# A joined fc1 chunk, a moved shared product and a reordered QR step in a four-layer block kernel

## The chip, the cores and the metric

The kernel runs on one core of a Trainium2 chip. The metric is the device time of one execution in microseconds (us). Before the change it is 1273.7, the median of three runs (1276.01, 1266.53, 1273.7).

The engines are named as in the profile: PE multiplies matrices and PEld loads its weights, DVE is the vector engine, ACT the scalar engine with its function tables, POOL is GpSimd, and SP issues DMAs. Each runs its instructions in program order and waits on semaphores for the others.

## What is computed

The input x is 32 samples of 128 tokens with 144 features, in f32; `c` is one vector of 144 per sample. Four layers follow each other:

```python
# layer 0: block with adaptive layernorm, q/k layernorm, 16 heads of 9
q, k = ln(q) * g_q, ln(k) * g_k
x = x + g_msa * (softmax(q k^T / 3) v @ w_proj + b_proj)
x = x + g_mlp * (gelu(xn2 @ w1 + b1) @ w2 + b2)        # 576 hidden
# layer 1: rotation
U, _ = qr(P)                                           # P is 144 x 64
R = expm(A(c))                                         # 64 x 64 skew matrix per sample
z = x @ U;  x = x + (z @ R - z) @ U^T
# layer 2: as layer 0, without the q/k layernorm
# layer 3: the same attention, then a mixture of four experts of 576 hidden
cw = softmax of the two largest of xn @ w_gate, else 0
x = x + g_mlp * sum_e cw[e] * (gelu(xn @ w1[e] + b1[e]) @ w2[e] + b2[e])
```

## The kernel before

In the code the blocks are numbered 0 to 2: block 0 is layer 0 ("L0"), block 1 is layer 2 ("L2"), block 2 is layer 3 ("L3"). All four experts are computed for all tokens, in two pairs.

**Tiling.** The 32 samples are 8 groups (NG) of 4 (G). x stays on chip. A contraction over 144 features is one matmul over 128 rows (the *main*) and one over the remaining 16 rows and the bias (the *rest*), which uses only a 32-row tile of PE's array. The rest's moving rows (hR) lie in four row groups, written there by two DMAs (hD, then hR), so that rests with different row tiles can run side by side. `both()` (L717) issues the mains and rests of a few output chunks, rests first or mains first, with a `yield` between the two halves, so that other work can be put there. It serves the q and k products (`qk_chunks`, L754, three chunks), the values, and the first product of each MLP (`fc1`, L1021, 128 of the hidden columns per chunk; five chunks in L0 and L2, nine for a pair of experts, where the last 64 columns of both experts share a chunk named SHARED). After a block of chunks `fc1` says the gelu function once, which loads ACT's table (L1035), and applies gelu to each chunk (L1038). The second product is `mlp2` (through `fc2`, L1044), one sample at a time. In the mixture of experts it is `moe2` and `moe2_parts` (L1204), and a product of the shared chunk (L1210) is done by one of the two experts of a pair for both; `shared_by_gate` multiplies that chunk by the tokens' gates first (L1176). These gates come as rows through a DMA (cwD to cwb), issued by `gate_rows_of` (L1186).

**Attention.** Scores are two products: one (ps_s) only for the row maxima nm (DVE L931), which PE transposes (L871); DVE then puts them beside q (L876), so that the second product (ps_w) comes with the maximum subtracted, and ACT takes its exponential (L935). PE weighs the values (L950), ACT copies the result "on" (L956), and the sums divide it: in blocks 1 and 2 by four DVE instructions (`sums_by_blocks`, L975 to L981), in block 0 by PE transposes and DVE (L963 to L993). Each sample has two halves of scores, n = 0 and n = 1. The scores, the chunks and the rest share seven PSUM banks in a ring; one more holds the weighed values.

**Order.** Nothing schedules at run time. A loop over *ticks* (L1455) advances each block by one sample, and the blocks overlap: block 0 starts at tick 0, block 1 at 35, block 2 at 67. Each tick has named *gaps* between its parts (a, e, t, stats, o, b0, b, den, pre1, c, y1, y2, y3, d, z). `put(tick, gap, f)` hangs work into a gap and `put2` the two halves of a `both` into two gaps (L1344 to L1432); t0 is the first tick of a group. In block 1, a group's MLP is put as three chunks into gap "c" of tick t0+8 and two chunks into gap "c" of t0+9, and mlp2 of its four samples into gaps "b" and "d" of t0+10 and "b" and "c" of t0+11. The q/k chunks of a group are put at its t0-2, gap "c", which is t0+10 of the group three before it. `fill` (L1441) is called at every gap. Besides what was put it runs the layernorm statistics (`ln_stats`, L659 and L660, followed by POOL's variance, L662 ff.), at gap "e" in the ticks of the first block, and two background generators: `prepare_qr` takes Householder QR columns step by step (PE L354, ACT L365, POOL L366, DVE L369 to L380), and `prepare_expm` the matrix exponentials, among them the eight DVE instructions of each half of the series (L568 to L570). The guess, at gap "e" too, is the start of Newton's iteration for the q/k layernorm (DVE L817 and L820, POOL L827 to L830). The residual of attention is formed by DVE (res_a, L1003) and added to x by POOL (L1000).

## Time and profile before

| | |
|---|---|
| median of three runs | 1273.7 us (1266.53 to 1276.01) |
| the profiled execution's own time | 1277.48 us |
| its span | 1275.8 us, mean granted PE clock 0.991 |
| PE busy | 1224.7 us, 13924 matmuls |
| DVE, ACT, POOL busy | 811.5, 781.1, 667.4 us |
| ACT table loads at L935 and L1035 | 57 and 58, 1283 ns each |
| DMA, mean over the span | 48 GB/s |

A profiled execution gives the start and length of every instruction. "Busy" is the time in which an engine has an instruction running; PE's matmuls are pipelined, so that two overlap and a matmul's length is more than its share of PE's time; the distance from one start to the next is that share. In rows of the timeline, "[2.16 <-DVE hid L1176]" says that the engine stood idle for 2.16 us ahead of this instruction, and that DVE's instruction on tile "hid" at line 1176 ended the wait. In rows of the windows, each engine's busy time is followed by its number of instructions, then the granted PE clock (1.00 is full), the share of the DMA engines and GB/s.

The block stages lie in the span as follows: block 0 alone to about 450, block 1 with the end of block 0 from there, blocks 1 and 2 together to about 800, block 2 alone after that, with the last group's experts from about 1200 on.

### The profile page before, as it was taken

How to read it: one execution, taken by the hardware profiler on the slowest of the kernel's cores; microseconds unless marked ns; L12 is line 12 of the kernel's file. 1: busy time of each engine (PE TensorE's matmuls, PEld its weight loads, DVE VectorE, ACT ScalarE, POOL GpSimd, SP SyncE). 2: the span in 40 equal slices, each digit the busy share in tenths (PEclk: the TensorE clock that was granted, in tenths of full speed). 3: DMA queues.
4: the chain of work that ended last, by engine and by line, in shares of the span. 5: the costliest groups of instructions: out<-in, count | busy, mean ns of one | idle time of the engine just before them, and what ended most of it. 6: DMA issues, size and time to landing. Idle time of an engine off the chain costs nothing.

```text
span 1275.8 us, 35335 instructions
## 1 busy us (share of the span) xinstructions
PE 1224.7 (96%) x13924; PEld 895.4 (70%) x13924; DVE 811.5 (64%) x2540; ACT 781.1 (61%) x1732; POOL 667.4 (52%) x1627
## 2 busy tenths in 40 slices
PE   6889898999989999999999999999999999999998
PEld 5668676778767677777777767767676767677666
DVE  4698888876775466676667666646464646455342
ACT  2567767678786665767666667555656565555441
POOL 5567776756664545454545454736362626261600
PEclk9999998999999999999999999999999999999999
DMA  8301011010013211111121111210101010110110
GB/s 220 84 3 38 2 37 37 2 38 18 23 36 124 60 42 38 46 55 35 50 86 55 56 38 47 103 55 27 55 27 55 27 55 30 53 37 17 37 36 17
DMA packets 53144, 60.74 MB, mean 48 GB/s; under 512 B 5200, under 2 KB 36560, under 8 KB 52720
## 3 DMA queue, kind: packets, MB, share of 16 engines
q1 hardware_dynamic: 52320, 58.01, 15.1%
q8 instruction: 112, 1.84, 0.6%
q10 hardware_dynamic: 656, 0.44, 0.2%
q14 instruction: 56, 0.46, 0.1%
HBM read 44.18 MB, written 13.07 MB: 45 GB/s over the span
## 4 chain that ended last, share of the span: by engine, by line
PE 67%; DVE 5%; ACT 1%; DMA 1%; issue 1%; POOL 0%; SPq 0%; DVEq 0%
PE ps_h L722 19%; PE ps_f L1204 9%; PE ps_s L919 6%; PE ps_w L919 6%; PE ps_o L950 6%; PE ps_qk L722 5%; PE ps_f L1044 4%; PE ps_pj L1014 3%; PE ps_v L722 3%; DVE nm L931 2%; PE ps_f L1210 1%; PE ps_o L871 1%; PE ps_hT_m L691 1%; PE ps_hT_a L691 1%; DVE block L979 0%
## 5 line engine op out<-in xcount | busy, mean ns | idle before, releaser
L931 DVE TENSOR_REDUCE nm<-ps_s 128x4 f32<-128x512 f32 x384 | 246.6, 683 | 93.7 <-PE ps_w L919 80.7
L935 ACT ACTIVATE pr<-ps_w 128x512 f32<-128x512 f32 x384 | 208.6, 595 | 145.5 <-PE ps_w L919 136.8
L919 PE MATMUL ps_s<-kT,qT 32*128 32x256 f32 (+2 forms) x1536 | 233.7, 407 | 0.9 <-ACT kT L851 0.9
L919 PE MATMUL ps_w<-q,kT 32*128 32x128 f32 x3072 | 232.5, 285 | 0.0
L919 PEld LDWEIGHTS ps_w<-q,kT 32*128 32x128 f32 x3072 | 196.6, 188 | 10.0 <-issue 6.3
L1038 ACT ACTIVATE hid<-ps_h 128x512 f32<-128x512 f32 (+1 forms) x224 | 120.5, 591 | 91.4 <-PE ps_h L722 91.0
L919 PEld LDWEIGHTS ps_s<-kT,qT 32*128 32x128 f32 x1536 | 137.3, 186 | 29.2 <-issue 9.4
L1214 DVE SCALAR_TENSOR_TENSOR acc<-ps_f,cwz,acc 128x144 f32<-128x144 f32 x128 | 46.7, 365 | 157.4 <-PE ps_f L1204 87.8
L722 PE MATMUL ps_h<-hM_m,mlps 128*128 128x512 f32 x304 | 144.1, 607 | 0.0
L1000 POOL TENSOR_TENSOR x_sb<-x_sb,res_a 128x144 f32<-128x144 f32 x96 | 47.1, 491 | 145.0 <-DVE res_a L1003 144.2
L950 PE MATMUL ps_o<-pr,vaug 128*32 128x128 f32 x3072 | 104.2, 276 | 0.0
L950 PEld LDWEIGHTS ps_o<-pr,vaug 128*32 128x32 f32 x3072 | 78.4, 110 | 32.7 <-PE ps_w L919 14.4
L722 PEld LDWEIGHTS ps_h<-hM_m,mlps 128*128 128x128 f32 x304 | 53.3, 189 | 67.0 <-issue 66.2
L1044 PE MATMUL ps_f<-mlps,hid 128*128 128x144 f32 x640 | 93.7, 294 | 0.0
L1044 PEld LDWEIGHTS ps_f<-mlps,hid 128*128 128x128 f32 x640 | 82.4, 190 | 8.8 <-issue 4.5
L935 ACT ACT_TABLE_LOAD x57 | 73.1, 1283 | 10.0 <-PE ps_w L919 9.1
L794 POOL TENSOR_SCALAR kT<-kT,cst 128x512 f32<-128x512 f32 x30 | 47.0, 1565 | 61.1 <-ACT kT L776 59.7
L662 POOL TENSOR_SCALAR rs_m_a<-mv_m_a 128x2 f32<-128x2 f32 x81 | 17.2, 212 | 114.2 <-DVE mv_m_a L660 86.3
L1204 PEld LDWEIGHTS ps_f<-mlps,hid 128*128 128x128 f32 x512 | 67.3, 190 | 13.5 <-issue 12.2
L1204 PEld LDWEIGHTS ps_f<-pair,hid 128*128 128x128 f32 x512 | 68.7, 193 | 9.7 <-issue 7.9
L1035 ACT ACT_TABLE_LOAD x58 | 74.4, 1283 | 1.0
L1204 PE MATMUL ps_f<-pair,hid 128*128 128x144 f32 x512 | 74.5, 292 | 0.0
(337 smaller groups left out, 2725.8 us busy)
## 6 DMA issues: line engine op xcount, KB each, us to landing
gates<-gates SPq DMA_DIRECT2D x48, 288.0 KB
hD_m<-hG_m SPq DMA_DIRECT2D x24, 256.0 KB
hR_m<-hD_m SPq DMA_DIRECT2D x24, 256.0 KB
hD_a<-hG_a SPq DMA_DIRECT2D x16, 256.0 KB
hR_a<-hD_a SPq DMA_DIRECT2D x16, 256.0 KB
cwb<-cwD SPq DMA_DIRECT2D x32, 128.0 KB
x_sb<-in_x SPq DMA_DIRECT2D x8, 288.0 KB
out_x<-x_sb SPq DMA_DIRECT2D x7, 288.0 KB
```

Of the source, the lines that this page charges most:

```text
L722: nc.tensor.matmul(ps, x, y, start=k == 0, stop=k == 1)
L794: eng.tensor_scalar(o, k, m, None, ALU.mult)
L919: nc.tensor.matmul(o, x, y, start=True, stop=True)
L931: nc.vector.tensor_reduce(to, view, AX.X, ALU.max, negate=True)
L935: nc.scalar.activation(pr[:, 4 * e : 4 * e + 4, :].rearrange("p s q -> p (s q)"), view, AF.Exp, scale=SCALE,)
L950: nc.tensor.matmul(po[rows4(j), t, :], v[:, 4 * j + 2 * t + r, :], prs[j // 2][:, 4 * (j % 2) + 2 * r + t, :], start=r == 0, stop=r == 1,)
L1000: nc.gpsimd.tensor_tensor(x_sb[:, b, :], x_sb[:, b, :], t, ALU.add)
L1035: nc.scalar.activation(t, half, AF.Gelu_apprx_tanh)
L1038: nc.scalar.activation(hid[:n, i], ps[:n], AF.Gelu_apprx_tanh)
L1044: nc.tensor.matmul(ps, hid[:, at0, i, :], w2[:, m, :], start=m == 0, stop=m == NFC - 1)
L1204: nc.tensor.matmul(ps[:, 0, :], hid[:, at0 + m, i, :], w2[:, at0 + m, :], start=m == 0, stop=m == 3)
L1214: nc.vector.scalar_tensor_tensor(acc, ps[:, 0, :], w, acc, ALU.mult, ALU.add)
```

## The change

It has three parts.

1. **First block.** The series' terms of the matrix exponential yield a mark. Where a mark comes at gap "z" of a tick, the next tick is put into `behind`: in that tick, gap "e" is left out, and its work (the statistics and the guess) runs at gap "t", where the pieces of the QR step have come first. This holds in eight ticks, those of QR columns 24, 26, and so on to 40. The instructions are the same; their order on DVE changes there.

2. **fc1 chunks.** A table, MLP_TILES, now gives the row tile of each chunk's rest. `both` has a third form (None): the first half of the mains, all rests, the second half of the mains. In block 1 four chunks are put at t0+8, gap "c", in this form; the fifth is joined with the three q/k chunks three groups ahead, in the same form, at t0+10, gap "c" (JOIN), with its gelu ahead of ACT's copies of q. Nothing is put at t0+9, gap "c". mlp2 goes from gaps b, d, b, c of ticks t0+10, 10, 11, 11 to gaps d, b, c, d of ticks t0+10, 11, 11, 11. In block 2 the second pair of the first five groups goes from 3+3+3 chunks to 4+4 and one that is joined with q/k chunks. All eight groups of block 1 have a joined chunk, which makes 13 joins. The gelu function is said before the products, in place of between them and the gelus, in this form.

3. **Last group.** For pair 0 of the last group the product of the shared chunk is done by the second expert for all four samples (before: by the first for three of them). `shared_by_gate` goes from gap "stats" to "den" there, and the DMA of the gate rows (`gate_rows_of`) from "den" to "pre1" for all groups.

The counts of instructions are the same but for ten more table loads. Weights are laid out on the host by MLP_TILES; that part of the diff is left out here.

```diff
--- before.py
+++ after.py
@@ -25,6 +25,10 @@
 
 SHARED = 8
 NPC = 9
+MLP_TILES = {
+    "L0": (0, 1, 2, 0, 1), "L2": (0, 1, 2, 3, 3),
+    "L3_0": (0, 1, 2, 0, 1, 2, 0, 1, 2), "L3_1": (1, 2, 3, 3, 0, 1, 0, 2, 3),
+}
 MLP_COLS = NFC * (128 + 128 + C)
 PAIR_COLS = NPC * (256 + C)
 D = 64
@@ -341,6 +345,7 @@
     rotU = const.tile([128, NB2, C], F32, name="rotU")
 
     qr_rest = 3 * D
+    SERIES = "series"
 
     def prep_qr():
 
@@ -565,10 +570,10 @@
             lo, hi = mat(f"{name}_lo"), mat(f"{name}_hi", "hi")
             for t, cs_ in ((hi, co[4:]), (lo, co[:4])):
                 nc.vector.tensor_scalar(t, pw1, cs_[1], None, ALU.mult)
-                yield
+                yield SERIES
                 for c, x in ((cs_[0], i2b), (cs_[2], pw2), (cs_[3], pw3)):
                     nc.vector.scalar_tensor_tensor(t, x, c, t, ALU.mult, ALU.add)
-                    yield
+                    yield SERIES
             yield from products(
                 pw4, hi, f"ps_{name}",
                 lambda bs, ps: nc.vector.tensor_tensor(lo[:, bs, :], lo[:, bs, :], ps, ALU.add),
@@ -716,7 +721,16 @@
 
     def both(main, rest, rest_first):
 
-
+        if rest_first is None:
+            n = len(main) // 2
+            for ps, x, y in main[:n]:
+                nc.tensor.matmul(ps, x, y, start=True, stop=False)
+            for k, (ps, x, y) in enumerate(rest):
+                nc.tensor.matmul(ps, x, y, start=k >= n, stop=k < n)
+            yield
+            for ps, x, y in main[n:]:
+                nc.tensor.matmul(ps, x, y, start=False, stop=True)
+            return
         for k, products in enumerate((rest, main) if rest_first else (main, rest)):
             for ps, x, y in products:
                 nc.tensor.matmul(ps, x, y, start=k == 0, stop=k == 1)
@@ -751,19 +765,31 @@
             gr[g]["kT"] = take_kT()
         return gr[g]["qT"], gr[g]["kT"]
 
+    JOIN = {(1, n): (1, n - 3) for n in range(3, NG)}
+    JOIN.update({(2, n): (1, n + NG - 3) for n in range(3)})
+    JOIN.update({(2, n): (2, n - 3) for n in range(3, NG)})
+
     def qk_chunks(g):
 
 
         p = PARAMS[g[0]]
         hM, hR = gr[g]["hM_a"], gr[g]["hR_a"]
         qT, kT = qk_tiles(g)
+        f = JOIN.get(g)
+        if f is not None:
+            l, mlp, m = ("L2", MLPS[1], 4) if f[0] == 1 else ("L3_1", PAIRS[1], 3)
+            name = f"{f[0]}_{f[1]}_s"
+            gelu_table(name, m)
+            psh, main, rest = fc1_products(f, l, mlp, name, (m,))
+        else:
+            main, rest = [], []
         pss = [bank([128, G * T], f"ps_qk_{g[0]}_{g[1]}_{m}") for m in range(3)]
         cols = [slice(128 * m, 128 * m + 128) for m in range(3)]
-        yield from both(
-            [(ps, p.wqk[:, c], hM) for ps, c in zip(pss, cols)],
-            [(ps, p.wqkR[rows4(m), cols[m]], hR[rows4(m)]) for m, ps in enumerate(pss)],
-            False,
-        )
+        main += [(ps, p.wqk[:, c], hM) for ps, c in zip(pss, cols)]
+        rest += [(ps, p.wqkR[rows4(m), cols[m]], hR[rows4(m)]) for m, ps in enumerate(pss)]
+        yield from both(main, rest, False if f is None else None)
+        if f is not None:
+            gelus(f, psh, (SHARED,))
         nc.scalar.copy(qT[:, 0, :], pss[0])
         if g[0] == 1 and g[1] < 2:
             nc.gpsimd.tensor_copy(kT[:, 3, :], kmask[:, 3:4].to_broadcast([128, G * T]))
@@ -1018,21 +1044,30 @@
         layer, b, g, i = of(s)
         residual(b, st[s].pop("pj"), gr[g]["ga"][:, i, :], f"a_{s}", layer == 0)
 
-    def fc1(g, p, name, m, to, rest_first):
-
+    def fc1_products(g, l, p, name, ms):
 
         hM, hR = gr[g]["hM_m"], gr[g]["hR_m"]
-        pss = [bank([128, G, T], f"ps_h_{name}_{m + i}") for i in range(len(to))]
-        cols = [slice(128 * (m + i), 128 * (m + i) + 128) for i in range(len(to))]
-        tiles = [rows4((m + i) % 3) for i in range(len(to))]
-        yield from both(
-            [(ps, p.w1[:, c], hM) for ps, c in zip(pss, cols)],
-            [(ps, p.w1R[r, c], hR[r]) for ps, c, r in zip(pss, cols, tiles)],
-            rest_first,
-        )
-
+        pss = [bank([128, G, T], f"ps_h_{name}_{m}") for m in ms]
+        cols = [slice(128 * m, 128 * m + 128) for m in ms]
+        tiles = [rows4(MLP_TILES[l][m]) for m in ms]
+        main = [(ps, p.w1[:, c], hM) for ps, c in zip(pss, cols)]
+        rest = [(ps, p.w1R[r, c], hR[r]) for ps, c, r in zip(pss, cols, tiles)]
+        return pss, main, rest
+
+    def fc1(g, l, p, name, ms, to, rest_first):
+        if rest_first is None:
+            gelu_table(name, ms[0])
+        pss, main, rest = fc1_products(g, l, p, name, ms)
+        yield from both(main, rest, rest_first)
+        if rest_first is not None:
+            gelu_table(name, ms[0])
+        gelus(g, pss, to)
+
+    def gelu_table(name, m):
         t = small.tile([128, 1], F32, tag="gelu", name=f"gelu_{name}_{m}", bufs=1)
         nc.scalar.activation(t, half, AF.Gelu_apprx_tanh)
+
+    def gelus(g, pss, to):
         for ps, i in zip(pss, to):
             n = 64 if g[0] < 2 and i == SHARED else 128
             nc.scalar.activation(hid[:n, i], ps[:n], AF.Gelu_apprx_tanh)
@@ -1045,7 +1080,8 @@
         return ps
 
     def mlp1(g, m, to, rest_first):
-        return fc1(g, MLPS[g[0]], f"{g[0]}_{g[1]}", m, to, rest_first)
+        ms = range(m, m + len(to))
+        return fc1(g, ("L0", "L2")[g[0]], MLPS[g[0]], f"{g[0]}_{g[1]}", ms, to, rest_first)
 
     def mlp2(g, i):
         b = g[1] * G + i
@@ -1166,8 +1202,11 @@
                 nc.gpsimd.tensor_tensor(acc, acc, t, ALU.add)
 
     def moe1(g, pair, part, rest_first):
-        to = ((0, 1, 2), (SHARED, 3, 4), (5, 6, 7))[part]
-        return fc1(g, PAIRS[pair], f"3_{g[1]}_{pair}", 3 * part, to, rest_first)
+        ms = range(3 * part, 3 * part + 3)
+        if part > 2:
+            ms = ((0, 1, 2, 4), (5, 6, 7, 8))[part - 3]
+        to = [(0, 1, 2, SHARED, 3, 4, 5, 6, 7)[m] for m in ms]
+        return fc1(g, f"L3_{pair}", PAIRS[pair], f"3_{g[1]}_{pair}", ms, to, rest_first)
 
     def shared_by_gate(g, pair):
 
@@ -1205,7 +1244,7 @@
                 ps[:, 0, :], hid[:, at0 + m, i, :], w2[:, at0 + m, :], start=m == 0, stop=m == 3
             )
         yield
-        shared = e % 2 == (i == 0)
+        shared = e % 2 == (i == 0 or (g[1], e // 2) == (NG - 1, 0))
         if shared:
             nc.tensor.matmul(
                 ps[:, 1, :], hid[:, SHARED, i, :], w2[:, SHARED, :], start=True, stop=True
@@ -1303,11 +1342,16 @@
         elif prep_last and next(prep_last, 0) == 0:
             load_late()
 
+    behind = set()
+
     def prepare_expm(tick, gap):
         nonlocal prep_expm
         if prep_expm and (tick >= 0 and gap in ("b", "z") or (tick, gap) == (-2, "z")):
             said = next(prep_expm, 0)
-            if said == 0:
+            if said is SERIES:
+                if gap == "z":
+                    behind.add(tick + 1)
+            elif said == 0:
                 prep_expm = None
             elif said is not None:
                 rot_T.append(said)
@@ -1399,27 +1443,31 @@
                     at_ = t0 + 12 + i // 2 + ((n, i) == (NG - 1, G - 1))
                     put(at_, "bd"[i % 2] if at_ < first[1] or (n, i) == (NG - 2, G - 1) else "bc"[i % 2], mlp2, g, i)
             elif layer == 1:
-                put2(t0 + 8, "c", "c", mlp1, g, 0, (0, 1, 2), True)
-                put2(t0 + 9, "c", "c", mlp1, g, 3, (3, SHARED), True)
+                put2(t0 + 8, "c", "c", mlp1, g, 0, (0, 1, 2, 3), None)
                 for i in range(G):
-                    put(t0 + (10, 10, 11, 11)[i], "bdbc"[i], mlp2, g, i)
+                    put(t0 + (10, 11, 11, 11)[i], "dbcd"[i], mlp2, g, i)
             else:
                 put2(t0 + 7, "o", "c", gate_logits, g)
                 put(t0 + 8, "e", expert_ranks, g)
                 put(t0 + 8, "stats", expert_weights, g)
                 put(t0 + 8, "den", gate_rows, g)
-                put(t0 + 9, "den", gate_rows_of, g, 1)
+                put(t0 + 9, "pre1", gate_rows_of, g, 1)
                 for i in range(G):
                     put(t0 + 8 + i // 2, "cdab"[i], moe_bias, g, i, n == NG - 1)
                 for pair in range(2):
                     at_ = t0 + 8 + 2 * pair
-                    put2(at_, "stats", "b0", moe1, g, pair, 0, True)
+                    if pair and n < NG - 3:
+                        put2(at_, "stats", "b0", moe1, g, pair, 3, None)
+                        put2(at_ + 1, "stats", "b0", moe1, g, pair, 4, None)
+                    else:
+                        put2(at_, "stats", "b0", moe1, g, pair, 0, True)
                     if n == NG - 1:
                         put2(at_, "stats", "pre1", moe1, g, pair, 1, True)
-                    else:
+                    elif not pair or n >= NG - 3:
                         put2(at_, "den", "pre1", moe1, g, pair, 1, False)
-                    put2(at_ + 1, "stats", "b0", moe1, g, pair, 2, True)
-                    put(at_ + 1, "stats", shared_by_gate, g, pair)
+                    if not pair or n >= NG - 3:
+                        put2(at_ + 1, "stats", "b0", moe1, g, pair, 2, True)
+                    put(at_ + 1, "den" if (n, pair) == (NG - 1, 0) else "stats", shared_by_gate, g, pair)
                     put2(at_, "y2", "y3", moe2_parts, g, 2 * pair, 0)
                     put(at_ + 1, "b", moe2, g, 2 * pair, 1)
                     put(at_ + 1, "c", moe2, g, 2 * pair, 2)
@@ -1445,7 +1493,12 @@
             prepare_qr(tick, gap)
             prepare_expm(tick, gap)
 
-        if gap == ("t" if tick < 0 else "e" if tick < first[1] else "stats") and tick in stats:
+        if gap == "e" and tick in behind:
+            return
+        if gap == "t" and tick in behind:
+            gaps[tick, "t"] = gaps.pop((tick, "e"), []) + gaps.pop((tick, "t"), [])
+        at_head = "t" if tick < 0 or tick in behind else "e"
+        if gap == (at_head if tick < first[1] else "stats") and tick in stats:
             ln_stats(stats.pop(tick))
         for f, args in gaps.pop((tick, gap), ()):
             f(*args)
...
```

## The prediction

> **What bounds the kernel now.** I read the page first: TensorE's share, then the chain of work that ended last.
>
> ```profile
> PE 1224.7 (96%) x13924; PEld 895.4 (70%) x13924; DVE 811.5 (64%) x2540; ACT 781.1 (61%) x1732; POOL 667.4 (52%) x1627
> ...
> PE 67%; DVE 5%; ACT 1%; DMA 1%; issue 1%; POOL 0%; SPq 0%; DVEq 0%
> ```
>
> 96% is an average, so next the windows by stage (length, then busy us of PE, PEld, DVE, ACT, POOL, granted clock, DMA):
>
> ```profile
> 50.00:250.00 200.00, 180.95 (x2414) 139.80 (x2413) 173.29 (x579) 139.14 (x402) 144.24 (x403) 0.97 0.09 27
> 250.00:450.00 200.00, 192.49 (x2612) 146.00 (x2612) 135.10 (x459) 145.16 (x363) 113.60 (x333) 0.98 0.15 48
> 450.00:600.00 150.00, 149.24 (x1876) 108.44 (x1874) 101.15 (x292) 96.35 (x189) 73.67 (x158) 1.00 0.15 44
> 750.00:1200.00 450.00, 447.88 (x4458) 317.85 (x4455) 247.47 (x735) 262.55 (x492) 221.26 (x461) 1.00 0.15 47
> ```
>
> From 450 on PE stands still for under 1%: there only less PE work can save, and every new wait of PE costs in full. In the first block DVE is the busier partner (87% in 50 to 250), and PE waits for it.
>
> Sums go against the profiled execution: 1277.48 us, span 1275.8, 3.8 above the median of 1273.7.
>
> **Part 1, layer 2's MLP on PE.** By starts in PE's rows, a 512-column main matmul is two passes of 0.43, a main-to-rest switch 0.52, rest matmuls of one row tile 0.52 a pass, and rests on other tiles follow 0.006 apart. So a fourth rest on a free tile is nearly free. Per group, before: three chunks 3.74, two chunks 2.88, the q/k chunks 4.04: 10.66. After: two blocks of four mains. One is 0.20 + 0.53 + 2 x 0.43 + 0.52 + 0.52 + 0.52 + 0.53 + 3 x 0.43 = 4.98, two are 9.96. PE work falls by 0.7 a group, 5.6 in eight.
>
> But the two-chunk block stood in gap "c" of tick t0+9, and nothing comes there now. Behind that gap PE transposes nm, the negated row maxima. This tick in group 2, PE's rows, then DVE's, then ACT's:
>
> ```profile
> 599.38 0.28 PE L919 MATMUL ps_w<-q,kT 32*128 32x128 f32 x2
> 599.49 1.02 PE L722 MATMUL ps_h<-hR_m,mlps 32*128 32x512 f32 x4
> 600.44 1.98 PE L722 MATMUL ps_h<-hM_m,mlps 128*128 128x512 f32 x4
> 602.26 0.27 PE L871 MATMUL ps_o<-cst,nm 128*128 128x128 f32 x1
> ```
> ```profile
> 598.27 0.45 DVE L975 STREAM_TRANSPOSE block<-on 128x256 f32<-128x256 f32 x1
> ...
> 599.86 1.28 DVE L931 TENSOR_REDUCE nm<-ps_s 128x4 f32<-128x512 f32 x2
> ```
> ```profile
> 595.60 1.28 ACT L935 ACT_TABLE_LOAD   x1 [0.85 <-PE ps_w L919]
> 596.89 1.09 ACT L935 ACTIVATE pr<-ps_w 128x512 f32<-128x512 f32 x2
> 597.86 0.38 ACT L956 COPY on<-ps_o 128x256 f32<-128x256 f32 x1
> ```
>
> The scores end at 599.4, nm at 601.14. The two chunks (599.49 to 602.26) hid that. The chain is table load, two exps, the copy of "on", four DVE instructions (1.6) and two reductions (1.28); the change shortens none of it. Without the chunks PE waits for it: from the end of the scores to the end of nm I read 1.76 in groups 0 to 3, 2.31 in group 4, and 2.72, 2.79, 2.79 in groups 5 to 7, where layer 3 shares the engines.
>
> The rest of the group: the chunk taken out returns as one more in tick t0+8 and one in t0+10 (counted above); the mlp2 steps move one gap later each, 1.23 out of t0+10 and into t0+11, net nothing. A 0.35 wait for q, seen now behind t0+8, is then covered. Lowest to highest the wait costs 0 (if nm is done with the scores) to 2.8; I take the readings.
>
> The joined chunk needs the q/k layernorm's transposed rows (hR_a, two DMAs on SP's queue). They land 1.4 to 2.9 before use (609.11 against 611.84, 753.84 against 755.26). In t0+10 the use comes 2.1 earlier: 1.24 of mlp2 is gone, and one main of 0.86 no longer lies ahead. ACT, which feeds it, is 0.3 to 0.6 earlier. So between 0 and 1.4 a group; I take 0.5.
>
> The first gelu of a joined chunk puts its table load and 0.59 of gelu ahead of ACT's copies of q: hidden while scores stand 2 us and more away, up to 1.3 a group if not. The exp load of t0+10 moves to t0+11, the same count in this layer.
>
> Per group: -0.7 + 1.76 - 0.35 + 0.5 + 0.1 = +1.3 in groups 0 to 3, +1.9 in group 4, +2.3 in 5 to 7. Sum **+14.0**.
>
> **Part 2, layer 3.** Five groups' second pair goes from 3+3+3 chunks to 4+4 and one joined. By the same passes 0.2 less each: **-1.0**. Its two more table loads a group (2.6 on ACT) lie in stretches where ACT is 58% busy; if they were bare, +13, if hidden 0; I take 0, since ACT waits 91 us for the chunks in front of its gelus.
>
> **Part 3, the first block.** In eight ticks (QR columns 24 to 40, every second) six DVE instructions of the QR step go ahead of two pairs of statistics and two of the guess. The tick of column 36, DVE, POOL, then PE:
>
> ```profile
> 210.11 0.30 DVE L1003 TENSOR_TENSOR res_a<-ps_pj,gates 128x144 f32<-128x144 f32 x1
> ...
> 211.77 0.15 DVE L369 SCALAR_TENSOR_TENSOR ala<-qrr,qr 128x1 uint32<-128x1 uint32 x1
> ```
> ```profile
> 210.49 0.49 POOL L1000 TENSOR_TENSOR x_sb<-x_sb,res_a 128x144 f32<-128x144 f32 x1 [0.23 <-DVE res_a L1003]
> 210.94 0.55 POOL L366 TENSOR_TENSOR qr<-qr,half 128x1 f32<-128x1 f32 x1
> ```
> ```profile
> 213.60 0.82 PE L354 MATMUL ps_qr<-at,cst 128*128 128x145 f32 x2 [2.44 <-DVE at L380]
> ```
>
> The step starts with L369, which needs POOL's power (L366). That stands in POOL's queue behind the residual add (L1000), which waits for DVE's res_a. It ends about 1.1 after res_a; the step starts 1.36 after it. The statistics and the guess (1.43) fill that hole. After the change the step can start only 0.27 earlier, DVE stands idle 1.1, and everything then behind the step (statistics, guess, the nm reductions, POOL's variance at L662) comes some 1.05 later, all queued on DVE. PE's next scores want the bank that nm frees: by each tick's slack PE loses 0.95, 0.6, 1.0, 1.09 and 1.09 in five, nothing in three: 4.7. PE's waits ahead of ps_qr (0.91, 1.93, 2.44 in three of these ticks) shrink by 0.27 each at most, which is within it. Bounds: -5.3 (all three waits gone) to +8.4 (1.05 in all eight). I take **+4.7**.
>
> **Part 4, the tail.** For the last group the shared product moves to the second expert, its gating to a later gap.
>
> ```profile
> 1242.50 0.51 PE L1210 MATMUL ps_f<-pair,hid 128*128 128x144 f32 x2 [2.16 <-DVE hid L1176]
> ```
> ```profile
> 1243.66:1247.07 3.41, 3.41 (x16) 3.41 (x15) 1.45 (x5) 0.00 (x0) 0.00 (x0) 0.50 0.23 82
> ```
>
> DVE's L1176 waited for the rows of cwb until 1241.75. Afterwards three first-expert products (0.98 each) fill the time, so the wait goes: -2.2. The half clock behind it (3.41 at 0.50, so 1.65 lost) should go too: **-3.8**. Next late is nothing that I see: the gated rows are then ready at 1242.4, before 1243.
>
> **The clock.** PE's rows show 0.50 for a 3.4 us window at 165.05, 212.84, 325.5, 383.5 and 1243.66, each after a window in which PE was busy for 1.25 to 1.87 of 3.41. A new wait of 1.8 to 2.8 in each of eight groups can do the same if it falls within one window; each costs 1.7 at most, all eight 13.6, none 0. I take two to three, **+4**, as only the larger waits reach it.
>
> The Trainium skill ("TensorE: Matmul & The Clock Gate", "Why this matters for your kernels") speaks of idle gaps of more than about 3 us; by that sentence no new wait here trips the clock, and the sum would be 4 lower, 1288. The trace disagrees: 0.50 followed single idle stretches of 1.9 to 2.4 us.
>
> **Sum.** 14.0 - 1.0 + 4.7 - 3.8 + 4 = +17.9. On 1277.5 that is 1295.4; less the 3.8 by which the profiled execution stands above the median, **1291.5**.
>
> **The rivals.**
> - *The gap costs nothing.* If nm were ready within 0.3 us of the scores in tick t0+9 (the DVE queue drained earlier, the exps earlier), the saved passes count in full: layer 2 -5.6, layer 3 -1, tail -3.8, first block 0 to +4.7: 1263 to 1268. It decides from a wait under 0.7. For it: DVE has 64% load overall. Against it: DVE's four block instructions and the reductions run back to back behind "on", without idle. Not slower. Chance 0.20.
> - *The first block's step helps.* The QR step starts earlier, PE's three waits go (-5.3) and nm is not late: 10 less than my sum, 1281.5. Against it: POOL's power is not earlier. As far as its start is concerned the change then does not do what it says. Chance 0.13.
> - *The clock drops in every tick t0+9*, and hR_a is late by 1.4 in all groups: +9.6 and +7.2, 1301 to 1308. For it: the waits are of the size that went before 0.50. Against: windows end anywhere in them. Chance 0.15.
>
> **How the numbers follow.** My own forecast has chance 0.52, with its own range 1284 to 1299. The range over all, 1267 to 1306, leaves out half of the first rival and the edge of the third. Under 1% a measurement of this kernel can hardly tell from no change: below 1261 is faster, above 1286.4 slower. Faster: the deep end of the first rival, 0.05. Within 1%: the rest of it, the second rival and the lower edge of my own, 0.35. Slower: 0.60.
>
> **What would show it.** Right: PE rows of the nm transpose (L871) in tick t0+9 waiting 1.6 to 2.8 for DVE L931; DVE idle about 1.1 ahead of L369 in the eight ticks; no wait at L1210; PE busy time some 5 lower and span higher. Wrong: L871 without a wait, or PE's ps_qr earlier by more than 0.3; a wait of ps_qk for hR_a above 1.4 would break the third term.

## The result

The changed kernel takes 1307.8 us (median of six runs, 1303.4 to 1313.3) against 1274.7 before (six runs, 1266.5 to 1276.3). The ratio is 1.0269, with a 95% interval of 1.0232 to 1.0305: it is slower by 30 to 39 us. The forecast was 1291.5 with a range up to 1306: the direction was right, the size was not.

The profiled execution after took 1313.3 (span 1311.6), 5.5 above its median. Its page:

```profile
PE 1233.3 (94%) x13924; PEld 898.3 (68%) x13924; DVE 809.2 (62%) x2540; ACT 800.2 (61%) x1742; POOL 666.6 (51%) x1627
...
PE 64%; DVE 5%; ACT 1%; issue 1%; DMA 1%; POOL 0%; DVEq 0%; SPq 0%
```

PE has the same 13924 matmuls, but its share fell from 96% to 94%: PE now waits. Its busy time rose by 9 although there is less to do, because matmuls last longer at half clock: a score matmul (ps_w) takes 0.27 us between 600 and 640, at full clock, and 0.42 in the half-clock stretch from 587 to 594. The windows of the stage where blocks 1 and 2 run (450 on), the first two with the joined chunks of layer 2, the third behind them:

```profile
450.00:600.00 150.00, 145.54 (x1645) 101.13 (x1644) 93.02 (x264) 91.78 (x177) 67.87 (x151) 0.98 0.16 48
600.00:840.00 240.00, 224.07 (x2805) 164.62 (x2804) 151.84 (x429) 153.14 (x288) 114.18 (x237) 0.98 0.17 50
850.00:1200.00 350.00, 349.65 (x3391) 245.84 (x3390) 186.29 (x557) 216.62 (x387) 170.76 (x358) 1.00 0.13 40
```

Before, PE was idle for 0.8 of 150 us in the first of them. Now it is idle for 4.5 of 150 and 16 of 240, and the clock is at 0.98. Behind layer 2 PE is full again.

To see where the time went, I compare the starts of the same instruction in both traces. PE transposes nm once per tick with scores, 96 times in all; the table gives by how much each start is later after the change.

| at the start of | before, us | after is later by |
|---|---|---|
| transpose 5 (ahead of the changed ticks) | 93.5 | 11.4 |
| transpose 29 (behind the first block's changed ticks) | 380.1 | 21.4 |
| transpose 37 (layer 2 has begun) | 482.2 | 19.8 |
| transpose 77 (layer 2 is done) | 878.4 | 41.3 |
| transpose 93 (before the tail) | 1131.8 | 40.0 |
| the end | 1275.8 | 35.8 |

So layer 2 lost 21.5, the first block's ticks 10, layer 3 gained 1.3 and the tail 4.2. The first 94 us lost 11.4, and nothing was changed there: PE's clock was at 0.50 from 30.8 to 68.3. The other kernels below have the same instructions up to there, and their profiled executions stand between 3.0 earlier and 9.3 later than that of before. This is the spread of single executions, not the change. In the first block the trace of before had 10.2 us at half clock in the changed ticks, that of after 3.4, so that the 10 is too little; the experiments take this out.

**Layer 2.** The same tick as in the prediction (group 2, t0+9), first PE's rows:

```profile
626.14 0.28 PE L945 MATMUL ps_w<-q,kT 32*128 32x128 f32 x2
628.12 0.30 PE L897 MATMUL ps_o<-cst,nm 128*128 128x128 f32 x1 [1.71 <-DVE nm L957]
```

then DVE's:

```profile
622.23 1.29 DVE L957 TENSOR_REDUCE nm<-ps_s 128x4 f32<-128x512 f32 x2 [0.75 <-PE ps_w L945]
...
625.04 0.45 DVE L1001 STREAM_TRANSPOSE block<-on 128x256 f32<-128x256 f32 x1
...
626.70 1.27 DVE L957 TENSOR_REDUCE nm<-ps_s 128x4 f32<-128x512 f32 x2
```

The wait that was forecast is there: 1.71 in groups 0 to 3, 2.18 in group 4, 2.65 to 2.67 in groups 5 to 7, 17.0 in all (I had read 17.7). The groups of the page for this line, before and after, show the whole of it:

```profile
L871 PE MATMUL ps_o<-cst,nm 128*128 128x128 f32 x62 | 18.3, 294 | 3.5 <-DVE nm L931 2.5
```
```profile
L897 PE MATMUL ps_o<-cst,nm 128*128 128x128 f32 x62 | 18.1, 292 | 20.8 <-DVE nm L957 20.6
```

Two of the windows around such waits (length, busy of PE, PEld, DVE, ACT, POOL, clock):

```profile
778.31:781.72 3.41, 0.80 (x22) 0.60 (x14) 3.20 (x10) 1.43 (x4) 2.61 (x6) 1.00 0.01 2
781.72:785.13 3.41, 3.37 (x24) 3.09 (x28) 0.73 (x2) 1.23 (x3) 0.49 (x1) 0.50 0.14 41
```

A window in which PE worked for 0.80 of 3.41 is followed by one at half clock. But not every wait has this after it. In groups 1 and 2 the wait is the same, 1.71, and PE works for 1.70 and 1.72 of the window; only group 1's is followed by half clock:

```profile
583.75:587.16 3.41, 1.70 (x33) 1.37 (x29) 2.84 (x6) 1.83 (x5) 2.35 (x6) 1.00 0.00 0
587.16:590.57 3.41, 3.41 (x20) 2.52 (x22) 1.65 (x6) 1.25 (x3) 0.00 (x0) 0.50 0.26 77
...
624.70:628.12 3.42, 1.72 (x34) 1.37 (x31) 3.04 (x8) 2.12 (x6) 2.61 (x6) 1.00 0.02 5
628.12:631.53 3.41, 3.40 (x52) 2.83 (x56) 1.94 (x7) 1.34 (x4) 0.49 (x1) 1.00 0.23 71
```

Layer 2 has 17 us at 0.50 after the change and had none before.

**The first block.** The tick of column 36, DVE's rows, then POOL's:

```profile
224.35 0.20 DVE L374 SCALAR_TENSOR_TENSOR ala<-qrr,qr 128x1 uint32<-128x1 uint32 x1 [1.10 <-POOL qr L371]
...
228.04 0.29 DVE L1029 TENSOR_TENSOR res_a<-ps_pj,gates 128x144 f32<-128x144 f32 x1
229.46 0.16 DVE L374 SCALAR_TENSOR_TENSOR ala<-qrr,qr 128x1 uint32<-128x1 uint32 x1 [1.12 <-POOL qr L371]
```
```profile
228.42 0.50 POOL L1026 TENSOR_TENSOR x_sb<-x_sb,res_a 128x144 f32<-128x144 f32 x1 [0.23 <-DVE res_a L1029]
228.87 0.56 POOL L371 TENSOR_TENSOR qr<-qr,half 128x1 f32<-128x1 f32 x1
```

The wait of 1.12 ahead of the moved step is the one that was forecast. But there is a second, 1.10, of which I had said nothing. It comes ahead of the step of column 35 (224.35), whose place in the program was not changed; a tick holds two columns. Behind this step stands oT on DVE, and PE's projection waits for oT:

```profile
226.07 0.76 PE L1040 MATMUL ps_pj<-L_wproj,oT 128*128 128x144 f32 x4 [2.37 <-DVE oT L1019]
```

**The tail.** PE goes through the first expert's products without a stop, and the wait of 2.16 is gone:

```profile
1276.48 2.84 PE L736 MATMUL ps_h<-hM_m,pair 128*128 128x512 f32 x6
1279.16 4.08 PE L1243 MATMUL ps_f<-pair,hid 128*128 128x144 f32 x32
1283.08 0.41 PE L1249 MATMUL ps_f<-pair,hid 128*128 128x144 f32 x2
```

The 4.2 is measured against an execution that had a half-clock window behind that wait. Of the eleven traces here with an unchanged tail seven have this window; in the four without it the tail is 1.6 to 2.0 shorter than before, so that against these the change gives 2.2 to 2.6.

### The profile page after: what moved, and what is told of

Read it like the earlier page. It is cut to its first block, busy times and chain, and to the rows that moved or that the text cites. A ratio compares the mean times of both kernels' runs of the same rounds, so it can differ in the third digit from the quotient of the medians.

```text
span 1311.6 us, 35352 instructions
## 1 busy us (share of the span) xinstructions
PE 1233.3 (94%) x13924; PEld 898.3 (68%) x13924; DVE 809.2 (62%) x2540; ACT 800.2 (61%) x1742; POOL 666.6 (51%) x1627
## 4 chain that ended last, share of the span: by engine, by line
PE 64%; DVE 5%; ACT 1%; issue 1%; DMA 1%; POOL 0%; DVEq 0%; SPq 0%
PE ps_h L736 11%; PE ps_f L1243 10%; PE ps_s L945 6%; PE ps_w L945 5%; PE ps_o L976 5%; PE ps_f L1079 4%; PE ps_pj L1040 3%; PE ps_h L732 3%; PE ps_h L727 3%; PE ps_v L736 2%; DVE nm L957 2%; PE ps_qk L732 2%; PE ps_h L729 2%; PE ps_f L1249 1%; PE ps_h_s L727 1%
## 5 line engine op out<-in xcount | busy, mean ns | idle before, releaser
L945 PE MATMUL ps_w<-q,kT 32*128 32x128 f32 x3072 | 236.1, 288 | 0.7 <-DVE nm L957 0.6
L1073 ACT ACTIVATE hid<-ps_h 128x512 f32<-128x512 f32 (+1 forms) x211 | 114.8, 595 | 68.2 <-PE ps_h L736 61.8
L1079 PE MATMUL ps_f<-mlps,hid 128*128 128x144 f32 x640 | 92.9, 292 | 0.0
L707 ACT ACTIVATE hM_m<-ps_hT_m,modM 128x128 f32<-128x128 f32 x96 | 44.5, 463 | 75.6 <-PE ps_hT_m L696 66.4
L667 POOL TENSOR_SCALAR rs_m_a<-mv_m_a 128x2 f32<-128x2 f32 x81 | 17.0, 210 | 139.5 <-DVE mv_m_a L665 91.6
L1243 PE MATMUL ps_f<-mlps,hid 128*128 128x144 f32 x512 | 72.8, 288 | 0.2 <-ACT hid L1073 0.2
```

What stands on the lines that cost most here:

```text
L945: nc.tensor.matmul(o, x, y, start=True, stop=True)
L1073: nc.scalar.activation(hid[:n, i], ps[:n], AF.Gelu_apprx_tanh)
L1079: nc.tensor.matmul(ps, hid[:, at0, i, :], w2[:, m, :], start=m == 0, stop=m == NFC - 1)
L1243: nc.tensor.matmul(ps[:, 0, :], hid[:, at0 + m, i, :], w2[:, at0 + m, :], start=m == 0, stop=m == 3)
```

## The experiments

Where a stage is compared, half clock has to be taken out first. The stretch from transpose 9 to transpose 23 holds the eight changed ticks (columns 24 to 30 and 34 to 40, every second; in the tick of column 32 nothing moves). Three kernels with the same instructions in it took 176.4 us with 10.2 at half clock (before), 173.6 with 3.4 (l3_tail) and 172.0 with none (tail_only): 0.43 us per us of half clock. Below, 172.0 is the stretch at full clock. For a kernel with another order in this stretch, taking off 0.43 is an estimate. "Measured" gives the ratio to the kernel before, with its 95% interval.

### The parts by themselves

The diffs here are against the changed kernel. The first block's reordering alone: layer 2, layer 3 and the tail are put back.

```diff
-    JOIN = {(1, n): (1, n - 3) for n in range(3, NG)}
-    JOIN.update({(2, n): (1, n + NG - 3) for n in range(3)})
-    JOIN.update({(2, n): (2, n - 3) for n in range(3, NG)})
+    JOIN = {}
...
-        shared = e % 2 == (i == 0 or (g[1], e // 2) == (NG - 1, 0))
+        shared = e % 2 == (i == 0)
...
-                put2(t0 + 8, "c", "c", mlp1, g, 0, (0, 1, 2, 3), None)
+                put2(t0 + 8, "c", "c", mlp1, g, 0, (0, 1, 2), True)
+                put2(t0 + 9, "c", "c", mlp1, g, 3, (3, SHARED), True)
...
-                    put(t0 + (10, 11, 11, 11)[i], "dbcd"[i], mlp2, g, i)
+                    put(t0 + (10, 10, 11, 11)[i], "bdbc"[i], mlp2, g, i)
...
-                    if pair and n < NG - 3:
+                    if pair and n < 0:
...
```

> The kernel before with the first block's reordering alone. Theory (stage by stage: first block +9.6, layer 2 +20.4, tail -4.2 in the two traces): +8 to +11 us over before, DVE idle about 1.1 us ahead of the QR step in the eight ticks and again ahead of the next column's step, PE waiting up to 2.4 us for oT ahead of the projection; layer 2, layer 3 and the tail as before. Rival (the loss came with a slow start of the profiled execution, 11.4 us in its first 70 us, and the clock, not with the order on DVE): 0 to +3 us, and the first block as long as before from the fourth tick on. My own prediction had +4.7.

Measured: 1.0098 (1.0060 to 1.0136), 1288.5 against 1276.6. The stretch is 186.3 with 3.4 at half clock, so 12.9 longer than before at full clock. In it DVE stood idle for 20.5 us ahead of QR steps; before, it never did. The loss belongs to the reordering, and 4.7 was far too little. PE's waits ahead of the projection, over the whole execution, first before and then in l0_only:

```profile
L1014 PE MATMUL ps_pj<-L_wproj,oT 128*128 128x144 f32 x256 | 45.4, 300 | 8.7 <-DVE oT L993 7.0 <-PEq L622 1.5
```
```profile
L1038 PE MATMUL ps_pj<-L_wproj,oT 128*128 128x144 f32 x256 | 45.3, 300 | 18.5 <-DVE oT L1017 16.1 <-PEq L627 1.4 <-ACT hid L1071 0.9
```

Layer 2's part alone: the first block is put back, and layer 3 and the tail as above.

```diff
-                if gap == "z":
-                    behind.add(tick + 1)
+                pass
...
-    JOIN.update({(2, n): (2, n - 3) for n in range(3, NG)})
```

> The kernel before with layer 2's joined chunk alone (four chunks in t0+8, none in t0+9, the fifth with the q/k chunks, mlp2 a gap later). Theory: +18 to +23 us, from PE idle ahead of the transpose of nm in t0+9 (1.7 us in groups 0 to 3, 2.2 in group 4, 2.7 in groups 5 to 7, 17 in all), some half-clock windows behind the larger waits (up to 7) and 0.7 us a group less PE work. Rival (the new order of mains and rests costs PE more than before): PE's starts in the joined blocks show over 10.7 us a group where 9.96 were worked out, and the waits for nm are smaller.

Measured: 1.0172 (1.0135 to 1.0209). Layer 2 is 22.6 longer, with 17.1 us at half clock. The joined block takes 5.0 where nothing is late (4.98 had been worked out), so the new order of mains and rests costs what it should.

Layer 3's part and the tail, then the tail alone, with the rest put back in the same way. In l3_tail this stays of the joins:

```diff
-    JOIN = {(1, n): (1, n - 3) for n in range(3, NG)}
-    JOIN.update({(2, n): (1, n + NG - 3) for n in range(3)})
+    JOIN = {}
     JOIN.update({(2, n): (2, n - 3) for n in range(3, NG)})
```

> The kernel before with layer 3's joined chunks (five groups) and the moved shared product, without the first block's and layer 2's parts. Theory: -3 to -5 us, nearly all in the tail, where PE's wait for the gated rows (2.16 us) and the half clock behind it go; layer 3 within 1 us of before. Rival (ten more table loads stand bare on ACT's path): layer 3 longer by 5 to 13 us, and the whole +1 to +9.

> The kernel before with the tail's part alone (shared product on the second expert, its gating later, the rows' DMA a gap later). Theory (PE's wait of 2.16 us for the gated rows goes, and the half clock behind it): -3.5 to -5 us, all of it behind the last group's scores. Rival (the later DMA of the rows in all groups makes the gating late in layer 3): layer 3 longer, whole 0 to +5.

Measured: l3_tail 0.9946 (0.9918 to 0.9973), tail_only 0.9953 (0.9923 to 0.9983). By the traces the tail gives 4.2 and layer 3 1.3, of which up to 0.3 stands in traces without layer 3's part too (the ratio of l3_tail stands for 3.4 to 10.5). The later DMA of the gate rows costs nothing: in tail_only the starts of layer 3's transposes move by less than 0.3 against before.

All but the first block's part:

```diff
-                if gap == "z":
-                    behind.add(tick + 1)
+                pass
```

> The whole change but for the first block's part. Theory (the parts add up: layer 2 +21, layer 3 and tail -6): +13 to +18 over before. Rival (the parts act on each other, or the whole change starts slower by some 8 us, since the three parts by themselves sum to 8 less than the change): +20 to +27.

Measured: 1.0144 (1.0115 to 1.0172). By ratios the three parts sum to 0.98 + 1.72 - 0.54 = 2.16%, two of them to 1.18%; the whole change measured 2.69 (2.32 to 3.05) and this one 1.44. The intervals overlap, so the parts add up as far as this can tell; a few us by which they act on each other are not excluded. In its profiled execution layer 2 is 24.9 longer, with 30.7 us at half clock (nine windows).

### What the first block pays for

From here on each diff is against the kernel with that part alone. First suspect: the step waits for a power that stands behind POOL's residual add. On l0_only, the add is issued later.

```diff
+        if tick not in behind:
+            while sums_later:
+                sums_later.pop()()
+        fill(tick, "a")
         while sums_later:
             sums_later.pop()()
-        fill(tick, "a")
```

> As l0_only, but in the eight ticks POOL's residual add is issued after the QR column's power instead of ahead of it. Theory (the moved step waits for a power that stands behind the residual add in POOL's queue): DVE's idle time ahead of the step falls from 1.1 to 0.3 to 0.5 us and the loss from about 9.6 to +2 to +5 us. Rival (it is the place of the statistics behind the step that costs, whatever the step waits for): the loss stays at +8 to +10.

Measured: 1.0089 (1.0058 to 1.0120). The first wait fell from 1.12 to 0.5 as expected, and little came of it: the stretch is 184.2 with 6.8 at half clock, 9.3 longer. What I took for the whole cause was less than a third of it. The second wait stayed. POOL's rows ahead of one such second wait, from l0_only, show why:

```profile
211.84 0.19 POOL L667 TENSOR_SCALAR rs_m_a<-mv_m_a 128x2 f32<-128x2 f32 x1 [2.63 <-DVE qky L841]
212.11 0.70 POOL L668 TENSOR_TENSOR rs_m_a<-rs_m_a,neghalf 128x2 f32<-128x2 f32 x1
212.79 0.19 POOL L669 TENSOR_SCALAR rs_m_a<-mv_m_a 128x2 f32<-128x2 f32 x1
213.09 1.82 POOL L674 TENSOR_SCALAR xh_m<-x_sb,rs_m_a 128x128 f32<-128x128 f32 x1
214.90 0.51 POOL L682 TENSOR_SCALAR xg<-x_sb,rs_m_a 128x16 f32<-128x16 f32 x1
...
217.30 0.55 POOL L371 TENSOR_TENSOR qr<-qr,half 128x1 f32<-128x1 f32 x1
```

POOL stands idle for 2.63 until the statistics have come (the row names qky, which ends in the same moment; but L667 reads the statistics, and starts 0.09 behind their end, as it did before the change). Then it goes through the layernorm and the four instructions of a Newton step, and only then takes the power of the next column, which ends at 217.85. DVE has waited 1.44 for it. Behind DVE's step stands oT, and PE's projection waits for that. So it should be the statistics that must not be late. Two runs ask this. In the first only the guess goes behind the step, and the statistics stay ahead of it:

```diff
+        at_head = "t" if tick < 0 else "e"
+        if gap == (at_head if tick < first[1] else "stats") and tick in stats:
+            ln_stats(stats.pop(tick))
         if gap == "e" and tick in behind:
             return
...
-        at_head = "t" if tick < 0 or tick in behind else "e"
-        if gap == (at_head if tick < first[1] else "stats") and tick in stats:
-            ln_stats(stats.pop(tick))
```

> The kernel before with half of the first block's part: in the eight ticks only the guess goes behind the QR step, the layernorm statistics stay ahead of it. Theory, mended after l0_pow_first (late statistics start POOL's layernorm chain late, and the next column's power stands behind that chain in POOL's queue, so that DVE and then PE's projection wait): the statistics fill DVE's hole again, no new wait ahead of the next column's step, first block within 2 us of before, whole -2 to +2. Rival (the guess, from which POOL's Newton steps start, is what must not be late): +6 to +12, as l0_only.

Measured: 1.0002 (0.9981 to 1.0022). The stretch is 172.4 with no half clock, the same as before; DVE's waits are gone. So it is the late statistics that cost, and not the late guess. In the second run the statistics stay late, but POOL's four normalizing instructions come behind the next column's power:

```diff
+        normals.append((pairs, rs))
+
+    normals = []
+
+    def normalize(pairs, rs):
         for k, (s, kind) in enumerate(pairs):
...
+        while normals and (gap == "den" or tick not in behind):
+            normalize(*normals.pop(0))
```

> As l0_only, but in the eight ticks POOL's four normalizing instructions (the long ones of the layernorm) are issued behind the next column's power instead of ahead of it. Theory (late statistics start POOL's chain late; the next column's power behind it makes DVE wait 1.1 to 1.4 us and PE's projection 2.4 to 2.7): that second wait of DVE shrinks to under 0.3 us, the projection's wait to about 1 us, and the loss from about 12 to +3 to +7; the first wait of 1.1 ahead of the step itself stays. Rival (the reductions of nm, 1.05 us later, are what PE loses, or the normalized rows are then late for their transposes): the loss stays at +8 or more, with PE waiting at the transposes or the scores.

Measured: 1.0090 (1.0055 to 1.0124). The second wait is gone and the projection's wait fell from 2.7 to 1.25, as expected, but the loss did not fall as far: the stretch is 190.1 with 20.5 at half clock, 9.3 longer at full clock, and the first wait had grown to 1.6 in three of the ticks and 2.7 in one. PE's waits for nm at the scores and transposes are all there: 5.2 in the stretch, 5.0 in l0_only, 0.9 before. So the rival was right in part. Both edits together:

> l0_pow_first and l0_split together: in the eight ticks the residual add comes behind the step's power and the four normalizing instructions behind the next column's power. In the stretch of these ticks DVE's idle time ahead of the QR steps was 20.5 us in l0_only, 14.4 in l0_pow_first and 12.0 in l0_split, with the stretch longer than before by 12.9, 9.3 and 9.3 (the clock's part taken out at 0.43 us per us of half clock). Theory (the loss is DVE's idle time ahead of the steps, from both powers): idle of 5 to 8 us, stretch +4 to +7, whole +4 to +8 over before. Rival (one of the two was only moved, and the late statistics cost 9 whatever POOL does): the stretch stays at +9 or more, with the wait at the scores or the transposes.

Measured: 1.0108 (1.0074 to 1.0141). The stretch is 185.0 with 13.7 at half clock, 7.1 longer at full clock, at the upper edge of what was expected for it; the whole is 12 us over before (1287.2 against 1275.2), well beyond the +4 to +8. The group lines of the step's first instruction (busy, mean ns, then the idle time ahead of it) for l0_only, l0_pow_first, l0_split, l0_both and l0_guess_only, in this order:

```profile
L374 DVE SCALAR_TENSOR_TENSOR ala<-qrr,qr 128x1 uint32<-128x1 uint32 x64 | 10.2, 160 | 32.3 <-POOL qr L371 32.3
```
```profile
L374 DVE SCALAR_TENSOR_TENSOR ala<-qrr,qr 128x1 uint32<-128x1 uint32 x64 | 12.4, 194 | 25.5 <-POOL qr L371 25.0 <-ACT hG_m L707 0.5
```
```profile
L374 DVE SCALAR_TENSOR_TENSOR ala<-qrr,qr 128x1 uint32<-128x1 uint32 x64 | 9.7, 152 | 22.9 <-POOL qr L371 22.9
```
```profile
L374 DVE SCALAR_TENSOR_TENSOR ala<-qrr,qr 128x1 uint32<-128x1 uint32 x64 | 12.0, 187 | 17.0 <-POOL qr L371 17.0
```
```profile
L374 DVE SCALAR_TENSOR_TENSOR ala<-qrr,qr 128x1 uint32<-128x1 uint32 x64 | 9.8, 152 | 9.2 <-POOL qr L371 9.2
```

In the stretch itself this idle time is 20.5, 14.4, 12.0, 7.9 and 0, and the stretch is longer by 12.9, 9.3, 9.3, 7.1 and 0.4. The loss falls with DVE's idle time ahead of the QR steps, but not in proportion. In l0_split and l0_both the projection's waits are nearly back at what they were (5.1 and 5.0 against 4.4), and what is left are PE's waits for nm, 5.2 and 5.1. This comes from profiled stretches and rests on the estimate of 0.43. By whole times l0_only and the three mended kernels can't be told apart (1.0089 to 1.0108). The mended ones had more half clock: over all their executions the granted clock is 0.990 on average in l0_only and 0.988, 0.987 and 0.986 in the three. Whether that is chance or comes from the edits was not shown. So the runs show that the late statistics cause the loss; how it divides among the two powers and nm is read from traces.

### What layer 2 pays for

Does the wait for nm begin at ACT's table load, as the prediction has it? The load is taken forward by a small exponential behind the gelus, on the kernel of l2_only.

```diff
         gelus(g, pss, to)
+        if l == "L2":
+            t = small.tile([128, 1], F32, tag="gelu", name=f"exp_{name}", bufs=1)
+            nc.scalar.activation(t, half, AF.Exp)
```

> As l2_only, with one small exponential said right behind the four gelus of a group, so that ACT's table load comes before the scores of t0+9 are done. Theory of the prediction (the chain to nm begins with ACT's table load, then two exponentials, the copy of on, DVE's block steps and reductions): the wait of PE for nm falls by 1.1 to 1.3 us a group, +8 to +12 over before. Rival (DVE itself is full from the first half's reductions on: reductions 1.29, statistics 0.93, copies of v 0.6, block steps 1.6, reductions 1.28, without a gap): the wait falls by no more than 0.3 us a group, and the whole stays at +17 to +21.

Measured: 1.0170 (1.0144 to 1.0195), no better than l2_only. The wait fell from 1.71 to 1.43 in groups 0 to 3 and not at all in most of the others, and in groups 0 to 3 the tick from one transpose of nm to the next grew from 8.41 to 9.06. ACT's two exponentials then start 0.4 instead of 1.4 behind DVE's first reductions, and DVE's rows show what holds nm:

```profile
602.02 1.29 DVE L956 TENSOR_REDUCE nm<-ps_s 128x4 f32<-128x512 f32 x2 [1.04 <-PE ps_w L944]
603.23 0.30 DVE L664 BATCH_NORM_STATS2 st_a<-x_sb 128x6 f32<-128x144 f32 x1
...
604.83 0.22 DVE L891 COPY vaug<-ps_v 128x72 f32<-128x72 f32 x1
604.97 0.43 DVE L1000 STREAM_TRANSPOSE block<-on 128x256 f32<-128x256 f32 x1
...
606.84 1.29 DVE L956 TENSOR_REDUCE nm<-ps_s 128x4 f32<-128x512 f32 x2 [0.20 <-PE ps_w L944]
```

From the first reductions to the second there is hardly a gap (0.45 of 4.82 us): reductions, statistics, four copies of v, four block steps, reductions. In l2_only, with the load where it was, DVE is idle for only 0.13 there, until ACT's copy of "on" has come. The rival holds. The size of the wait was read rightly; its chain was only one of two that end together, and the other is DVE's own queue. The edit is no clean test of the load's price: ACT's copies (hM_m, xM, xR) now stand behind the load, and the scores end 0.9 later in the tick.

Next, the gap is filled with work of no use, which keeps PE busy and brings nm no earlier:

```diff
+    def keep_busy(g):
+        hM = gr[g]["hM_m"]
+        ps = bank([128, G * T], f"ps_busy_{g[1]}")
+        nc.tensor.matmul(ps, MLPS[1].w1[:, :128], hM, start=True, stop=True)
+        nc.tensor.matmul(ps[:, : 2 * T], MLPS[1].w1[:, 128:256], hM[:, :2, :], start=True, stop=True)
...
+                put(t0 + 9, "c", keep_busy, g)
```

> As l2_only, with two matmuls of no use (512 and 256 columns, some 1.6 us, their result is not read) put into the empty gap of t0+9, so that PE waits under 0.3 us in groups 0 to 3 and some 1.2 us in 5 to 7, while nm comes no earlier. Theory (a part of layer 2's loss is the half clock that follows the idle stretches, about 1.5 us for each window of 3.4): no half-clock window in layer 2 and the loss from +21 to +13 to +17. Rival (the clock windows do not come from these waits): the windows stay and the loss is +20 to +24.

Measured: 1.0103 (1.0063 to 1.0142). Layer 2 has no half clock at all and is 15.3 longer instead of 22.6. So 7.3 of layer 2's loss was the clock, for 17.1 us at 0.50 in l2_only: 0.43 per us again. Another pair gives less: the whole change and no_l0 have the same instructions in layer 2, and no_l0 is 3.4 longer there (24.9 against 21.5) for 13.6 us more at half clock, 0.25 per us.

Then useful work: two chunks in t0+8, two in t0+9, the fifth joined.

```diff
-                put2(t0 + 8, "c", "c", mlp1, g, 0, (0, 1, 2, 3), None)
+                put2(t0 + 8, "c", "c", mlp1, g, 0, (0, 1), None)
+                put2(t0 + 9, "c", "c", mlp1, g, 2, (2, 3), None)
```

> As l2_only, with the four chunks split into two in t0+8 and two in t0+9, so that PE has 2.9 us of work again while nm is made; the fifth chunk stays joined. Theory (the empty gap is what costs, the saved passes are small): no wait for nm above 0.3 us in t0+9, no half-clock window in layer 2, the wait in t0+8 up by less than 0.5; layer 2 at 0 to +4 of before. Rival (the joined chunk, or mlp2 a gap later, costs by itself, through hR_a or the gelus ahead of q's copies): layer 2 stays at +8 or more.

Measured: 1.0065 (1.0041 to 1.0090). The waits and the half clock are gone, but layer 2 is still 11.0 longer: half of the rival was right. The joined block takes 5.4 to 7.0 in its groups, and PE's rows name what is late:

```profile
641.92 1.12 PE L729 MATMUL ps_h_s<-hR_m,mlps 32*128 32x512 f32 x2
643.94 1.14 PE L729 MATMUL ps_qk<-hR_a,L_wqkR 32*128 32x512 f32 x6 [0.90 <-DMA hR_a<-hD_a]
```

If hR_a is what is late, two more mains ahead of the rests should cover it:

```diff
-        yield from both(main, rest, False if f is None else None)
+        yield from both(main, rest, False)
```

> As l2_two_two, but in the joined block all four mains come first and the four rests last. In l2_two_two PE has work while nm is made, and layer 2 is still 11 longer; the joined block takes 5.0 us where nothing is late and 5.4 to 7.0 in its groups, 9.4 us over in all. Theory (this is hR_a landing after PE's first half of mains): with two more mains of 0.86 ahead of the rests the excess falls to 1 to 4 us and layer 2 to +2 to +6. Rival (the joined block is slow in itself, or waits for a PSUM bank): the excess stays at 7 or more.

Measured: 1.0036 (1.0012 to 1.0061). The joined block takes 4.90 to 4.96 in all eight groups, and layer 2 is 5.5 longer than before. It was hR_a. PE's rows of the same group:

```profile
642.34 2.74 PE L736 MATMUL ps_qk<-hM_a,L_wqk 128*128 128x512 f32 x6
645.01 0.69 PE L736 MATMUL ps_h_s<-hR_m,mlps 32*128 32x512 f32 x1
645.02 0.71 PE L736 MATMUL ps_qk<-hR_a,L_wqkR 32*128 32x512 f32 x3
```

The 5.5 that stays is not from PE's waits for nm, which are those of before (3.0 against 2.3). The two-chunk blocks take 3.28 each in the new form and 2.88 with the rests first (0.8 a group, 6.4 in eight).

### What paid, together

Layer 3, the tail and the guess alone behind the step:

> Layer 3's joined chunks and the tail, with only the guess behind the QR step: what paid or cost nothing in the runs so far. Theory: as l3_tail, -4 to -10 us. Rival (the guess behind the step gives PE's waits for the QR column back, 0.9 to 2.4 us in three ticks): 3 to 5 us below l3_tail.

Measured: 0.9964 (0.9938 to 0.9990), not better than l3_tail or tail_only. The three can't be told apart. The best that these parts give is 0.3 to 0.8% below before, nearly all of it from the tail.

## Why the prediction missed

By terms, against the traces:

| term | predicted | found |
|---|---|---|
| layer 2 without the clock | +14.0 | +14.2 (21.5 less 17.1 us at 0.50 times 0.43) |
| the clock there | +4 | +7.3 |
| first block | +4.7 | +12.6 (186.1 with 3.4 at half clock, against 172.0) |
| layer 3 | -1.0 | -1.3 |
| tail | -3.8 | -4.2 |
| sum | +17.9 | +28.6 |

The split of layer 2's 21.5 goes by the price 0.43; at the 0.25 of no_l0 it is 17.2 and 4.3. The sum is the same.

**Layer 2** held in its parts: PE idle 17.0 of 17.7 read from the trace of before, the joined block 5.0 for 4.98, the late hR_a 3.6 in all (joined blocks above 5.0) for 4. What it named as the chain, from ACT's table load on, was only one of two: in l2_exp_early, with the load taken forward, DVE's own queue brings nm no earlier. The reading of the wait did not depend on it.

**The failing step** is the first block's: "everything then behind the step ... comes some 1.05 later", of which only PE's wait for the bank of nm was priced, at 4.7 with an upper bound of 8.4. That price was about right: PE's waits for nm in the stretch are 5.0 in l0_only and 0.9 before. The step also started 0.25 earlier, for 0.27 forecast. The prediction names POOL's variance (L662) among what is late and stops there. Followed on, POOL's queue leads to the power of the next column, from there to DVE's next step, to oT and PE's projection: a second stall in the same tick, which was put at nothing. PE's waits ahead of the projection rose from 4.4 to 14.5 in the stretch, twice what was priced. The second rival was right in one thing: PE's waits ahead of ps_qr did fall, from 5.7 to 1.4 in l0_only, more than the 0.27 each that the prediction allowed. PE's idle time in the stretch rose by 9.5 in all; where the rest of the 12.9 lies is not shown.

**The clock** was taken at two to three windows; there were five of 3.4 us, and nine in no_l0 with the same instructions in layer 2. They came behind waits of 1.7 as well as 2.7, which was the rule that failed: that only the larger waits reach it. The prediction's reading of the trace before was too narrow as well. The half clock at 383.5 followed a window in which PE was busy for 2.14, outside its 1.25 to 1.87, with no single wait above 0.8. The page "TensorE: Matmul & The Clock Gate" of the Trainium skill ("Why this matters for your kernels") speaks of gaps of more than about 3 us. The runs go against it as a limit: in group 1's tick a window with PE busy 1.70 of 3.41 was followed by 0.50, and filling the waits (l2_busy) took every such window away. Nor is there a limit in PE's share of one window: 1.72 in group 2 was not followed by 0.50.

**What stays open.** The sum found is 28.6, the measured difference 30 to 39. The profiled execution after also lost 11.4 in its first 94 us, by chance as far as the other profiles show. Of the changed kernel's other five runs only the time and the granted clock are known: 0.977 to 0.985, where the kernel before has 0.991 to 0.992 on average in the runs beside the experiments. A us at 0.50 takes half a us off the mean, so that is some 28 us more at half clock than before, 17 of which lie in layer 2 in the profiled execution. At 0.43 the other 11 would be 5 us, an estimate, which would close the gap to the 33 between the medians; where they lie is not known. How far the parts act on each other is open within the intervals of no_l0.

The forecast's own range (1284 to 1299) was thus too low by the first block and the clock, and the range over all ended 2 us below the median. The 14.0 for layer 2 without the clock came out so closely in part by luck, since the price that separates the clock is itself between 0.25 and 0.43.

## What to carry to other kernels

A step that is moved forward runs no earlier than its latest input; look up in which queue that input's producer stands, and what the moved step now makes late in that same queue. Follow each delayed instruction through every engine until it meets the next step of the same loop: here the second round gave PE twice the waits of the first. Before a gap in PE's program is emptied, see what was being made behind it, and expect a stretch at half clock behind many of the new waits (here five to nine windows for eight waits).

## What was not expected of the hardware

POOL's normalizing instruction (128x128) takes 0.45 us in all 28 cases between 130 and 310 us before the change. In l0_only five of the 28 run beside DVE's 1024-wide series instruction (L575, 1.21 us, two inputs from SBUF), and those five take 1.82; none of the other 23 is above 0.55. But the meeting itself is not new. Before the change the same DVE instruction met a shorter one of POOL, on the same way to the next power, which takes 0.22 elsewhere (217.82):

```profile
214.94 1.27 DVE L570 SCALAR_TENSOR_TENSOR hid<-pow,hid 128x1024 f32<-128x1024 f32 x1
```
```profile
215.22 1.06 POOL L829 TENSOR_SCALAR qkh<-qkh 128x32 f32<-128x32 f32 x1
```

With 0.14 more on the row ahead of it (L828) that cost some 1.0 there, and the meeting in l0_only costs 1.4. In the tick of column 36 the time from one power of POOL to the next grew from 5.7 to 8.6; some 0.4 of this is the moved meeting, and 2.5 is POOL's longer wait for the statistics (2.63, before 0.14). The Trainium skill ("GPSIMD Engine Reference", "1. Specifications") says that POOL's SBUF interfaces are shared with VectorE and that they contend where DVE has two SBUF inputs, which fits; these rows show what it costs here.

A us at half clock cost 0.43 us in the first block's stretch and 0.25 to 0.43 in layer 2, less than the 0.5 that would be lost if nothing but PE's work set the time.
